# Rounding, routing and turned maxima reordered in a one-core attention and mixture-of-experts kernel

## The chip, the core and the metric

The kernel runs on one core of one Trainium2 chip. A core has five engines that run beside each other, each in the order of its own queue: PE (TensorE, matrix products and transposes), DVE (VectorE), ACT (ScalarE), POOL (GpSimd) and SP (which here only issues transfers). They hand work to each other through semaphores. SBUF is the working memory, PSUM the small memory that PE writes to.

The metric is the device time of one execution in microseconds (us), as the median of several. The profile comes from one execution of its own.

## What is computed

The input is `x`, 16 sequences of 256 tokens with 128 channels, 4096 tokens in all. Cut to what matters:

```python
xn = layernorm(x)                                  # over the 128 channels, eps 1e-5
# attention on xn: 16 heads of 8 channels
Q, K, V = relu(xn @ Wq + bq), relu(xn @ Wk + bk), relu(xn @ Wv + bv)
key_mask = sign(abs(sum(xn, -1)))                  # 0 where the channels sum to exactly 0
scores = einsum(Q, K) / sqrt(8)
scores = where(key_mask == 0, NEG, scores); scores = where(causal, scores, NEG)
a = softmax(scores) * key_mask_of_the_query
o = a @ V + xn
attn = gamma * (o - mean(o)) / sqrt(var(o) + 1e-8) + beta
# experts on xn: 8 experts, 448 hidden channels, the best two per token
h = rms_weight * xn * rsqrt(mean(xn * xn) + 1e-6)
top_w, top_i = top_k(softmax(h @ gate_w.T), 2)     # renormalised over the two
moe = xn + sum over the two of top_w * (silu(h @ w1.T) * (h @ w3.T)) @ w2.T
out = x + attn + moe
```

The mask asks whether a sum of 128 normed values, in the reference's own rounding, is exactly zero. So the kernel must know the normed values bit by bit for it, as an exactly rounded quotient.

## The kernel before, in words

**Tiles and blocks.** 128 tokens are a tile (32 of them, `NT`), four tiles are a block (8 of them, `NB`), which is two sequences. `y` (L103) holds first the input, then the centred input, then the exactly rounded quotient, and at last the attention's output; `xn` (L102) holds the normed values.

**The order of the work.** PE's order is the order of the program, since PE is scheduled by hand (L98). For DVE, ACT and POOL the compiler's scheduler orders the instructions at compile time: an instruction that is ready by its model may be placed ahead of one that stands earlier in the program.

**Norm.** Means are summed in `mean_of` (L306), for the first block on DVE, for the others on POOL. `normed` (L317) works on three chunks of 4, 12 and 16 tiles (L78): it centres on ACT (L325), squares and sums by a scan on DVE (L332, L334), takes a square root by Newton steps (L259), scales on ACT (L361), and refines the root (L365 to L382).

**Exact rounding.** `exact` (L385) makes the rounded quotient of a block from split products: it cuts the value in two halves (L398 on DVE; L401 on `eng`), forms three products by twelve ACT instructions (L407), the residue on DVE (L412), adds the products (L417 on `eng`), and corrects (L421 on DVE). `eng` is DVE for block 0 and POOL for the others. Then it sums the channels of all its blocks in the reference's order (`lane_sum`, L283), and writes the masks `off_all` and `on_all` (L427, L428). It is called for block 0, block 1, and then for pairs of blocks.

**Routing.** `logits` (L548) transposes `xn` and multiplies by the gate. `route` (L432) ranks the experts of each token, finds each token's place in its expert's list, and writes the rows to lists in HBM by indirect DMAs from POOL (L536), 64 in all, in three waves of 16, 8 and 8 tiles (L79). `planned` (L819) computes which expert tile of 256 rows is worked when.

**Attention.** `projected` (L569) makes K, Q and V of a block. The first product into K's PSUM tile is followed by one with `diag` (L579 on ACT, L584 on PE), a diagonal of the mask, so K of a block needs that block's mask. A unit is one block and half its heads, 16 units in all (L619). `scores` (L621) forms the scores in three parts (PE L635, L648), and DVE reduces each to its maxima (L658, L666). `queries` (L680) transposes the maxima and adds them to Q (PE L685, DVE L687, ACT L690, the tile `Qm`). `weights` (L695) forms the scores again, transposed and shifted (PE L710, L723), and ACT takes the exponential (L731). `values` (L734) multiplies by V (PE L743, L754; copied by ACT L764), `finish` (L767) divides and adds (DVE L776 to L810).

**Experts.** `experts` (L900) works 36 tiles in the main part; each fetches 256 rows of a list and its weights through SP (L924 to L934) and takes four steps: two `up` (PE L952, ACT L960, DVE L961 and L963), `down` (PE L969, ACT L977) and `deliver` (PE L983, DVE L985, two indirect DMAs from POOL at L989).

**The main loop** (L1110) traces unit u in an order written out by hand: weights of u, scores of u+1, values and finish of u, and between them six calls of `fill` (L1087). A `fill` advances the generator `prepared` (norm, exact rounding and routing, L1059) by three steps or up to a PAUSE, the projection of the next block by `k_next` steps, the experts by 1.55 steps in the mean (from unit 3 on, L83), and the closing norm (`rest`, L1029) by one. At the end of a unit come `values` of the second sequence, `queries` of the next unit, and `finish`; the next unit's first weights follow directly. After the loop the left experts and the closing norm are worked (L1151 to L1157), and the experts' results are fetched back and added (L1173 to L1185). The pool `psM` (L121) has two PSUM buffers that the projections, logits, transposes, values and expert results share; `psS` (L120) has six for scores, weights and the experts' `up`.

Of the kernel before, what the change touches and what calls it, by code (L numbers as in the profile page):

```python
# [26 lines left out]
def tile_attention_plus_moe(  # L27
# [55 lines left out]
    EARLY_STEPS, EXPERT_STEPS, EXPERTS_FROM = 3, 1.55, 3  # L83
# [233 lines left out]
    def normed(t0, t1):  # L317
# [60 lines left out]
        ninv = small.tile([P, nt], F32, tag="ninv", name=f"ninv_{n}")  # L378
        V.reciprocal(ninv, root)
        V.tensor_scalar(ninv, ninv, -1.0, None, ALU.mult)  # L380
        rhi, rlo = high_low(root[:], nt, "quot")
        roots[t0] = rhi, rlo, ninv  # L382
        yield

    def exact(c0, t0, t1, eng):  # L385

        rhi, rlo, ninv = roots[c0]
        n = f"x{t0}"  # L390
        for b in range(t0, t1, BT):
            bs = slice(b, b + BT)
            q, d = xn[:, bs, :], y[:, bs, :]
            i0 = b - c0
            qh = norm.tile([P, BT, C], F32, tag="qh", name=f"qh_{b}")
            ql = norm.tile([P, BT, C], F32, tag="ql", name=f"ql_{b}")
            r = norm.tile([P, BT, C], F32, tag="r", bufs=2, name=f"r_{b}")
            V.tensor_scalar(  # L398
                qh.bitcast(U32), q.bitcast(U32), HI_BITS, None, ALU.bitwise_and
            )  # L400
            eng.tensor_tensor(ql, q, qh, ALU.subtract)  # L401
            ps = []
            for k, (half, by) in enumerate(((qh, rlo), (ql, rhi), (ql, rlo))):
                p = norm.tile([P, BT, C], F32, tag=f"p{k}", name=f"p{k}_{b}")
                for t in range(BT):
                    i = i0 + t
                    S.activation(p[:, t, :], half[:, t, :], AF.Copy, scale=by[:, i : i + 1])  # L407
                ps.append(p)
            yield
            for t in range(BT):  # L410
                i = i0 + t
                V.scalar_tensor_tensor(  # L412
                    r[:, t, :], qh[:, t, :], rhi[:, i : i + 1], d[:, t, :], ALU.mult, ALU.subtract
                )
            yield
            for p in ps:
                eng.tensor_tensor(r, r, p, ALU.add)  # L417

            for t in range(BT):
                i = i0 + t  # L420
                V.scalar_tensor_tensor(  # L421
                    d[:, t, :], r[:, t, :], ninv[:, i : i + 1], q[:, t, :], ALU.mult, ALU.add
                )
            yield
        tot = small.tile([P, t1 - t0], F32, tag="tot", name=f"tot_{n}")
        yield from lane_sum(tot, y[:, t0:t1, :], t1 - t0, f"s{n}", V)
        V.tensor_scalar(off_all[:, t0:t1], tot, 0.0, None, ALU.is_equal)  # L427
        V.tensor_scalar(on_all[:, t0:t1], off_all[:, t0:t1], -1.0, 1.0, ALU.mult, ALU.add)  # L428
        exact_upto[0] = t1 // BT
        yield  # L430
# [138 lines left out]
    def projected(n):  # L569
# [6 lines left out]
        diag = qkv.tile([P, BT, P], BF16, tag="diag", name=f"diag_{n}")  # L576
# [4 lines left out]
        for r in range(NR):  # L581
# [15 lines left out]
            yield  # L597
            qp = misc(f"q_ps_{n}_{r}")
            T.matmul(qp, lhsT=wq_sb[:, r, :], rhs=xnT, start=True, stop=True)
            QT = qkv.tile([P, BW], F32, tag="QT", bufs=2, name=f"QT_{n}_{r}")  # L600
            S.activation(QT, qp, AF.Relu, bias=qb_sb[:, r : r + 1], scale=QSCALE)
            state[n, r] = (QT, KT, KTm)
            yield
        for b in range(2):
# [16 lines left out]
    def scores(u, part):  # L621
# [21 lines left out]
        for g in range(NG):  # L643
# [13 lines left out]
            if part == 2:  # L657
                V.tensor_reduce(  # L658
# [5 lines left out]
                )  # L664
            else:
                V.tensor_reduce(  # L666
# [5 lines left out]
                )  # L672
# [22 lines left out]
    def weights(u, part):  # L695
# [22 lines left out]
        for g in range(NG):  # L718
# [12 lines left out]
            S.activation(e[:, g, :], sp[g], AF.Exp)  # L731
# [327 lines left out]
    def prepared():  # L1059

        routed = 0
        for a, z in CHUNKS:
            eng = V if a == 0 else G
            yield from normed(a, z)

            first = min(a + BT, z) if a < 2 * BT else a
            if first > a:
                yield from exact(a, a, first, eng)
# [10 lines left out]
            for b in range(first, z, 2 * BT):  # L1079
                yield from exact(a, b, min(b + 2 * BT, z), eng)  # L1080

    exact_upto = [0]
    early_work = prepared()
    side = {"experts": iter(()), "rest": iter(()), "next": iter(())}
    due = [0.0]

    def fill(k_next=1):  # L1087

        for _ in range(EARLY_STEPS):
            if next(early_work, None) is PAUSE:  # L1090
                break
        for _ in range(k_next):
            next(side["next"], None)
        due[0] += EXPERT_STEPS
        while due[0] >= 1:
            next(side["experts"], None)
            due[0] -= 1
        next(side["rest"], None)
# [6 lines left out]
    for _ in projected(0):  # L1105
        pass
# [3 lines left out]
    for u in range(len(units)):  # L1110
        n, r = units[u]
        more = u + 1 < len(units)
        if r == 0 and n + 1 < NB:
            while exact_upto[0] < n + 2:
                next(early_work)
            side["next"] = projected(n + 1)
# [3 lines left out]
        fill()  # L1120
        if more:
            if r == 1:
                while (units[u + 1]) not in state:
                    next(side["next"])
            scores(u + 1, 0)
        fill()
        weights(u, 1)
        fill()
        if more:
            scores(u + 1, 1)  # L1130
        fill(r)
# [3 lines left out]
        fill(r)  # L1135
        weights(u, 2)
        finish(u, 0, o0)
        fill(r)
        if r == 1:
            for _ in side["next"]:  # L1140
                pass
        o1 = values(u, 1)
        if more:
            queries(u + 1)
# [93 lines left out]
```

## Time and profile before

| what | before |
|---|---|
| time, median of 3 runs | 728.03 us (725.95 to 730.34) |
| time of the profiled execution | 728.52 us |
| its span | 726.7 us |
| mean granted PE clock | 0.916 |
| busy: PE, PE weight loads | 566.6 us (78%), 339.6 us (47%) |
| busy: DVE, ACT, POOL | 459.8 (63%), 324.2 (45%), 251.3 us (35%) |
| DMA, mean | 70 GB/s, 50.82 MB |
| share of the chain that ended last: PE, DVE, ACT, POOL | 52%, 20%, 8%, 7% |

The span is the time from the first to the last record of the profiled execution; its own time is measured around it. Busy time is the union of an engine's instructions. The page cuts the span into 40 slices and shows for each the busy tenths of an engine. The clock is the share of full speed that PE was granted. A wait is named by the waiting engine and line and by the line that released it. The chain follows the last instruction back, at each step to what released it.

### The profile page before, as it was taken

The page shows a single profiled execution, that of the slowest core. Times are in us where ns is not written, and L with a number is a line of the kernel's source. Part 1 is how long each engine was busy: PE and PEld are TensorE (multiplying, and loading weights), DVE is VectorE, ACT ScalarE, POOL GpSimd, SP SyncE. Part 2 cuts the span into 40 slices and gives each one's busy share as a digit, 9 for nine tenths or more (in the row PEclk, how much of TensorE's full clock was granted, in tenths as well). Part 3 has the DMA queues.
Part 4 walks back from the last instruction along what each step waited for, and adds up shares of the span by engine and source line. Part 5 has one row for each costly group of instructions (what it writes and reads, how often), then busy time and mean ns, then how long its engine had stood idle before and what let it go on. Part 6 is the DMA issues. An engine that isn't in the chain of part 4 may idle for free.

```text
span 726.7 us, 10435 instructions
## 1 busy us (share of the span) xinstructions
PE 566.6 (78%) x3387; PEld 339.6 (47%) x3401; DVE 459.8 (63%) x1236; ACT 324.2 (45%) x708; POOL 251.3 (35%) x321
## 2 busy tenths in 40 slices
PE   0128778489587898989898989898989899898950
PEld 0013434244354555655455655565555565566740
DVE  5999878976257776655367736564576564637425
ACT  1557755334431634443444553544364444344310
POOL 8404634268814856521121411221142112213630
PEclk9995558889978999999999999999999999999985
DMA  6000000011160225422132211321222122223319
GB/s 160 1 0 0 1 0 1 0 38 38 44 197 27 76 77 147 129 75 67 40 95 64 68 53 54 104 70 45 69 63 83 53 64 75 81 68 91 105 41 329
DMA packets 40761, 50.82 MB, mean 70 GB/s; under 512 B 5925, under 2 KB 33073, under 8 KB 40705
## 3 DMA queue, kind: packets, MB, share of 16 engines
q1 hardware_dynamic: 32128, 38.11, 18.1%
q0 software_dynamic: 4352, 8.47, 3.6%
q10 hardware_dynamic: 4224, 3.55, 1.6%
q8 instruction: 28, 0.46, 0.3%
q14 instruction: 29, 0.23, 0.1%
HBM read 38.35 MB, written 12.27 MB: 70 GB/s over the span
## 4 chain that ended last, share of the span: by engine, by line
PE 52%; DVE 20%; ACT 8%; POOL 7%; issue 6%; DMA 5%; another core or an unknown queue 0%; DVEq 0%; SPq 0%; POOLq 0%; ACTq 0%
PE A L952 7%; PE Y L969 7%; PE G L952 7%; PE S L635 6%; PE W L710 6%; PE O L743 4%; PE W L723 4%; PE S L648 3%; POOL lists L536 3%; ACT e L731 2%; ACT Qm L690 2%; DVE tops L666 2%; DVE y L421 2%; PE O L754 2%; DVE r L412 2%
## 5 line engine op out<-in xcount | busy, mean ns | idle before, releaser
L989 POOL DMA_INDIRECT places<-fres,frows x72 | 70.5, 979 | 272.1 <-DVE fres L985 234.7
L731 ACT ACTIVATE e<-W 128x512 f32<-128x512 f32 x192 | 99.0, 601 | 64.1 <-PE W L723 64.1
L961 DVE SCALAR_TENSOR_TENSOR th<-th,A 112x512 f32<-112x512 f32 x72 | 49.1, 683 | 93.9 <-ACT th L960 93.9
L666 DVE TENSOR_REDUCE tops<-S 128x2 f32<-128x512 f32 x128 | 79.3, 681 | 20.4 <-PE S L648 20.2
L710 PE MATMUL W<-Qm,KT 32*128 32x512 f32 (+1 forms) x512 | 63.0, 569 | 27.8 <-ACT Qm L690 25.2
L952 PE MATMUL A<-hT,w 128*112 128x256 f32 x288 | 78.2, 395 | 7.9 <-ACT hT L943 6.8
L635 PE MATMUL S<-KTm,QT 32*128 32x256 f32 (+1 forms) x512 | 73.3, 560 | 6.0 <-DVE tops L666 4.9
L952 PE MATMUL G<-hT,w 128*112 128x256 f32 x288 | 75.5, 385 | 0.0
L969 PE MATMUL Y<-hid,w 112*128 112x256 f32 x288 | 70.5, 388 | 0.4 <-DVE hid L963 0.4
L536 POOL DMA_INDIRECT lists<-rows_c,ratu_c x64 | 62.4, 975 | 18.5 <-issue 14.4
L960 ACT ACTIVATE th<-A 112x512 f32<-112x512 f32 x72 | 43.4, 602 | 46.6 <-PE A L952 46.6
L952 PEld LDWEIGHTS A<-hT,w 128*112 128x112 f32 x288 | 48.8, 181 | 25.5 <-ACT hT L943 11.0
L969 PEld LDWEIGHTS Y<-hid,w 112*128 112x128 f32 x288 | 54.5, 194 | 11.4 <-issue 1.9
L952 PEld LDWEIGHTS G<-hT,w 128*112 128x112 f32 x288 | 52.0, 181 | 11.8
L764 ACT COPY oT<-O 128x512 f32<-128x512 f32 x32 | 18.8, 586 | 78.1 <-PE O L754 78.1
L963 DVE TENSOR_TENSOR hid<-th,G 112x512 f32<-112x512 f32 x72 | 49.4, 686 | 6.5 <-PE G L952 0.6
L710 PEld LDWEIGHTS W<-Qm,KT 32*128 32x128 f32 x512 | 25.5, 200 | 43.9 <-ACT Qm L690 28.8
L635 PEld LDWEIGHTS S<-KTm,QT 32*128 32x128 f32 x512 | 32.5, 196 | 26.3 <-issue 10.9
L417 POOL TENSOR_TENSOR r<-r,p 128x512 f32<-128x512 f32 x21 | 28.1, 1337 | 43.0 <-DVE r L412 19.5
L658 DVE TENSOR_REDUCE tops<-S 128x4 f32<-128x512 f32 x64 | 39.7, 682 | 3.7 <-PE S L648 3.6
L723 PE MATMUL W<-cmask,ident_bf 128*128 128x256 bf16 (+1 forms) x192 | 41.8, 346 | 0.0
L743 PE MATMUL O<-e,vstat 128*32 128x512 f32 x256 | 38.0, 619 | 2.0 <-ACT hT L943 0.8
(240 smaller groups left out, 880.9 us busy)
## 6 DMA issues: line engine op xcount, KB each, us to landing
w<-in_w1T_dram SPq DMA_DIRECT2D x36, 224.0 KB, 2.6
w<-in_w3T_dram SPq DMA_DIRECT2D x36, 224.0 KB, 3.5
w<-in_w2T_dram SPq DMA_DIRECT2D x36, 224.0 KB, 3.5
frows<-lists SPq DMA_DIRECT2D x36, 130.0 KB, 2.0
x<-in_x_dram SPq DMA_DIRECT2D x8, 256.0 KB, 4.0
z<-places ACTq DMA_DIRECT2D x4, 512.0 KB, 9.4
z<-places SPq DMA_DIRECT2D x4, 512.0 KB, 10.2
lists<-filling SPq DMA_DIRECT2D x9, 130.0 KB, 4.1
```

What stands on the lines that cost most here:

```text
L536: ins = G.indirect_dma_start(out=lists, out_offset=bass.IndirectOffsetOnAxis(ap=at_u[:, r, b + t : b + t + 1], axis=0), in_=rows[:, t, :], ...
L635: T.matmul(out, lhsT=QT[rows, q0 : q0 + P], rhs=KTm[rows, :, b * SEQ : b * SEQ + nk], start=(part < 2 or b == 0), stop=False, skip_group_c ...
L666: V.tensor_reduce(top[:, part, 1, cols], sp[g].rearrange("p (j k) -> p j k", j=HG), AX.X, ALU.max, negate=True,)
L710: T.matmul(out, lhsT=KT[rows, k0 : k0 + P], rhs=Qm[rows, :, k0 : (b + 1) * SEQ], start=(part > 0 or b == 0), stop=False, skip_group_check= ...
L723: T.matmul(out, lhsT=ident_bf, rhs=cmask[:, 1, :].unsqueeze(1).to_broadcast([P, 4 if part == 0 else 2, P]), start=False, stop=True, skip_g ...
L731: S.activation(e[:, g, :], sp[g], AF.Exp)
L743: T.matmul(op[rows, :], lhsT=v[:, 2 * b, r * NG + g, :], rhs=e0[:, g, :], start=True, stop=False, skip_group_check=True, tile_position=(0, ...
L952: T.matmul(to[:, ts(c, SL)], lhsT=wt[:, 0, ts(2 * k + c, CI)], rhs=hT, start=True, stop=True,)
L961: V.scalar_tensor_tensor(th, th, 1.0, ap, ALU.add, ALU.mult)
L963: V.tensor_tensor(h, th, gp, ALU.mult)
L969: T.matmul(yp, lhsT=w2[:, 0, c, :], rhs=hid[c // 2][:, ts(c % 2, SL)], start=(c == 0), stop=(c == NCI - 1),)
L989: ins = G.indirect_dma_start(out=places, out_offset=bass.IndirectOffsetOnAxis(ap=rows[:, a, C : C + 1].bitcast(U32), axis=0), in_=res[:, a ...
```

## The change

It has five parts. (1) `exact` works one block at a time, wholly on DVE and ACT, in eight steps, and forms sum and mask of each block by itself; block 0 still comes first, blocks 1 to 7 are a separate generator `masks`, advanced by two steps a `fill` as soon as their norm is traced, and brought up to block n+1 in unit (n, first half) after the first `values`. The roots that it reads are kept in constants. (2) `beside` traces steps of `prepared` and `masks` inside `tc.issue_after(...)`: each DVE or ACT instruction of such a step is ordered after the last one noted in `behind`, which is the last reduction of `scores` on DVE and the last exponential of `weights` on ACT (at first the last of `exact(0)`). (3) `projected` forms Q ahead of K and of the mask's diagonal; its steps are spread over the two units of a block by the list `due_next`. (4) `queries` of the next unit stands ahead of `values` of the second sequence, with a seventh `fill` after them. (5) The experts take 1.65 steps a `fill`, from unit 4 on.

```diff
-    EARLY_STEPS, EXPERT_STEPS, EXPERTS_FROM = 3, 1.55, 3
+    EARLY_STEPS, EXPERT_STEPS, EXPERTS_FROM = 3, 1.65, 4
...
-    def exact(c0, t0, t1, eng):
...
+    behind = {}
+
+    def exact(n):
+        bs = ts(n, BT)
+        q, d = xn[:, bs, :], y[:, bs, :]
+        by = [roots[n * BT + t] for t in range(BT)]
...
+        V.tensor_scalar(qh.bitcast(U32), q.bitcast(U32), HI_BITS, None, ALU.bitwise_and)
+        V.tensor_tensor(ql, q, qh, ALU.subtract)
+        yield
+        ps = []
+        for k, (half, j) in enumerate(((qh, 1), (ql, 0), (ql, 1))):
+            p = norm.tile([P, BT, C], F32, tag=f"p{k}", name=f"p{k}_{n}")
             for t in range(BT):
+                ins = S.activation(p[:, t, :], half[:, t, :], AF.Copy, scale=by[t][j]).ins
+            ps.append(p)
+        if n == 0:
+            behind["ACT"] = ins
+        yield
+        for t in range(BT):
+            V.scalar_tensor_tensor(
+                r[:, t, :], qh[:, t, :], by[t][0], d[:, t, :], ALU.mult, ALU.subtract
+            )
+        yield
+        for p in ps:
+            V.tensor_tensor(r, r, p, ALU.add)
+        yield
...
+        for k, _ in enumerate(lane_sum(tot, d, BT, f"s{n}", V)):
+            if k % 4 == 3:
+                yield
+        V.tensor_scalar(off_all[:, bs], tot, 0.0, None, ALU.is_equal)
+        ins = V.tensor_scalar(
+            on_all[:, bs], off_all[:, bs], -1.0, 1.0, ALU.mult, ALU.add
+        ).ins
+        if n == 0:
+            behind["DVE"] = ins
+        exact_upto[0] = n + 1
+        yield
...
+        QT = q_of(0)
+        diag = qkv.tile([P, BT, P], BF16, tag="diag", bufs=1, name=f"diag_{n}")
...
+            if r + 1 < NR:
+                QT = q_of(r + 1)
+                yield
...
+        behind["DVE"] = ins
...
+            ins = S.activation(e[:, g, :], sp[g], AF.Exp).ins
+        behind["ACT"] = ins
...
+            normed_upto[0] = z // BT
+            if a == 0:
+                yield from exact(0)
...
+    masks = chain(*(exact(n) for n in range(1, NB)))
...
+    def beside(work):
+        with ExitStack() as order:
+            for ins in behind.values():
+                order.enter_context(tc.issue_after(ins))
+            return next(work, None)
+
+    def fill(k_next=0, k_masks=2):
         for _ in range(EARLY_STEPS):
-            if next(early_work, None) is PAUSE:
+            if beside(early_work) is PAUSE:
                 break
+        for _ in range(k_masks):
+            if exact_upto[0] < normed_upto[0]:
+                beside(masks)
...
-    for _ in projected(0):
-        pass
+    for k, _ in enumerate(projected(0)):
+        if k > 3:
+            beside(early_work)
...
+        due_next = [0, 0, 0, 0, 1, 1, 1] if r == 0 else [1, 1, 1, 1, 0, 0, 0]
...
         o0 = values(u, 0)
-        fill(r)
+        if r == 0 and n + 1 < NB:
+            while exact_upto[0] < n + 2:
+                beside(masks if normed_upto[0] > n + 1 else early_work)
+            side["next"] = projected(n + 1)
+        fill(due_next[4])
         weights(u, 2)
         finish(u, 0, o0)
-        fill(r)
-        if r == 1:
-            for _ in side["next"]:
-                pass
-        o1 = values(u, 1)
         if more:
             queries(u + 1)
+        fill(due_next[5])
+        o1 = values(u, 1)
         exps.pop((u, 0))
+        fill(due_next[6])
         finish(u, 1, o1)
```

## The prediction

> **What bounds the kernel now.** I read the slices of the span first, then the busy time by stage, the waits, the chain that ended last, and single unit ends in the timeline. A unit is one pass over one block and half its heads; sixteen follow each other, and a unit starts when its Qm is written.
>
> The slices (18.2 us each) show three stages. PE is nearly idle for 55 us, then busy at half to 0.9 clock until about 200 us, then busy 8 to 9 tenths at full clock until 700 us, and 26 us of result fetching follow.
>
> ```profile
> PE   0128778489587898989898989898989899898950
> DVE  5999878976257776655367736564576564637425
> PEclk9995558889978999999999999999999999999985
> ```
>
> By stage, with sums of 100, 40 and 349 us (start:end, length, then busy PE, PEld, DVE, ACT, POOL and the clock):
>
> ```profile
> 60.00:160.00 100.00, 74.06 (x337) 37.53 (x341) 85.25 (x240) 54.88 (x153) 43.72 (x38) 0.69 0.02 5
> 160.00:200.00 40.00, 29.59 (x218) 15.31 (x212) 17.64 (x50) 18.98 (x35) 32.73 (x46) 0.97 0.13 42
> 285.00:634.00 349.00, 319.72 (x2060) 192.55 (x2069) 200.80 (x461) 163.41 (x323) 81.02 (x79) 0.98 0.26 75
> ```
>
> From 60 to 160 us DVE is the busy engine (85%); from 285 us PE is (92%). The waits (total, times, longest) name the holes:
>
> ```profile
> PE W L710 <- ACT Qm L690: 25.2, 15, 6.0
> PE k_ps L584 <- ACT diag L579: 18.2, 1, 18.2
> PE hT_ps L941 <- DMA frows<-lists: 7.8, 1, 7.8
> ```
>
> The first comes at every unit's end, 16.4 us in twelve times after 230 us: PE waits 1.4 us for the turned maxima. The second is the start: the first K matmul needs the mask column. The chain says why that is late; between two links of the mask's sum stand squares and scans of later blocks:
>
> ```profile
> 42.35 0.14 DVE lacc_sx L290
> 42.48 0.08 DVE yv_c L349
> 42.56 1.13 DVE xn L334
> 43.69 0.08 DVE lh_sx L294
> 43.77 0.08 DVE yv_c L350
> 43.86 0.59 DVE sq_c L332
> ```
>
> [...] the trace has 677 ns for the adds of L417 on DVE, and 1337 ns on POOL. [...] L421 takes 334 ns at best, 596 ns in the mean and 1417 ns at worst, always beside a POOL add. [...]
>
> **Prices of the stages.** Qm starts at 78.70, 135.30, 165.88, 187.80, 243.10 and 284.84 us (units 0 to 5), and at 633.61 us for unit 15. So units 5 to 14 take (633.61-284.84)/10 = 34.9 us. In the tail an expert tile takes 6.22 us (682.20, 688.42, 694.64 are starts of successive Y). A unit carries 6 fills x 1.55 / 4 = 2.33 tiles = 14.5 us, so attention alone is 20.4 us; unit 2 without experts took 21.9. Check: 243.1 + 12 x 20.4 + 33.7 tiles x 6.22 + 25.5 us from the last yT to the end = 723.0; 3.7 us are left over to the span of 726.7.
>
> **The change, part by part.**
>
> *Mask of block 0 undisturbed.* The sum and mask of L288 to L427 took from 36.03 to 46.68 us. The same sum alone, for the mean, ran from 4.46 to 7.07 us; with one mask operation 2.8 us. Gain 7.9 us, and 1.0 us at L417, whose adds waited behind a scan (31.14 to 32.88): the diagonal starts near 37.8 instead of 46.7 us. From there to the first scores were 10.9 us. Q placed first hides its matmul (-1.5), vb no longer waits 2.2 us in DVE's queue, the logits' transposes and matmuls now stand there (+3): 10.2, hence 48.0 us. From the first scores to Qm were 21.1 us, in which reductions, minima and Qs stood 5.8 us behind norm work: 15.3. Unit 0 starts near **63 us** instead of 78.7.
>
> *What is put off.* The norm of blocks 1 to 7 filled DVE from 30 to 62 us; it now falls into units 0 to 3, at three steps a fill. I count what those units must do on DVE, back to back as the chain shows it, and, as upper end, with the latencies of single instructions. Attention, each unit: 12 reductions x 0.60, rows of finish 1.8, norm sums 1.1, Qs, KTm, vb 1.4: 11.5 to 12.9 us. The norm of blocks 1-3: three squares and scans x 1.74 + some 35 small ones: 11 to 12.8; of blocks 4-7: 13.5 to 15. Exact rounding, a block: 0.34 + 1.05 + 1.05 + sum and mask 2.0 = 4.4, and what comes from POOL, 0.60 + 3 x 0.65 = 2.55: 7.0 to 7.7; at two steps a fill 5.5 blocks are done by unit 4: 38.5 to 42. Routing of 16 tiles 12 to 13.8, of 8 tiles 7 to 8, two plans 7 to 8, logits 0.6. Sum 136 to 152, taken **144 us**. At 0.87 busy (0.85 before, less the holds by POOL) that is 166 us. PE has 4 x 20.4 + 13 for logits = 95 us at full clock; at 0.69 that is 138, so it fits beside. Unit 4 starts at 63 + 166 = **229 us**; before it was 243.1, with 2.3 tiles done.
>
> *POOL to DVE.* POOL loses 28 operations (28.1 + 8.9 us), DVE gains 7 x 2.55 = 17.9 us, counted above. What it saves is DVE time held: L412 and L421 are 12 us over 64 x 0.31, the ranks' L455 to L457 about 3, single small ones some 7. This is why 136 to 152 us are enough for what took longer.
>
> *Routing queued behind.* Every instruction traced beside waits in DVE's or ACT's order for the last reduction or exponential. Behind the waiting ones stand PE's transposes of the next block (in order on PE) and the two shared PSUM buffers, which are freed by lraw (PE stood 3.0 us on it at 105 us). That is in the 0.87. On POOL the 32 list writes with their rows took from 149.97 to 199 us; the weights of the rows are now due in the fourth fill of unit 1, near 130 us, so the lists stand at about 180. SP's first fetch is queued at unit 4, 229 us: the 7.8 us wait goes, and its cover is 50 us. The second and third wave are due in units 3 and 4, the tiles that read them (9 and 17) in units 7 and 9.
>
> *Maxima one group ahead.* A fill and the second values matmuls (3.5 us) now stand between queries and the unit's first weights. The chain from PE to Qm is 2.8 us (319.15 to 321.95), so it is covered; if Qs stood behind a full group of reductions (2.48 us), just so. With oT's wait of 0.4 us, which the last fill covers, a unit loses 1.8 us: **18.6 us**.
>
> *Seven fills of 1.65.* 2.89 tiles a unit; 12 units hold 34.7, so all tiles cost PE 6.22 us as before and only the place moves. The last norm, which lay under 40 us of tiles, lies under 8 us now: bounds 0 and 4 us, taken 0, since the z fetch of 5 us follows. Buffers of one for r and diag, and constants for the roots, cost nothing: their readers are done a unit earlier, else 0.4 us a block.
>
> *Sum.* 229 + 12 x 18.6 + 36 x 6.22 + 25.5 + 3.7 + 7 = 712. The 7 us are unit 4, where DVE has about 44 us (attention 12, tiles 9, 1.5 blocks 11, routing 12) against 36.6 of PE. The profiled run took 728.52 with a span of 726.7, so 1.8 us lie around it: **714 us**; that run is 0.5 us over the median.
>
> **Rivals.**
> 1. The start is given back. With single-instruction latencies (152 us) and 0.85 busy the first units take 179 us, unit 4 starts at 242: 727 us, no change. For it: DVE idles from 37 to 63 us, where it worked before. Against: no holds by POOL.
> 2. Slower. PE stays at half clock while DVE is full, each waiting for the other in order, and experts begin a unit later, so nothing else fills PE. Units of 50 us (unit 0 took 56.6) put unit 4 at 263: 748 us. It decides from 184 us for units 0 to 3 on. Against: most of unit 0's length was norm work of all blocks and POOL holds.
> 3. The order does not do what it says: the compile-time order moves early work or finish before Qs, and the 1.8 us of 12 units stay (+22): 736 us.
>
> **How the numbers follow.** My forecast has 0.58, its own range 695 to 724 (142 to 176 us for units 0 to 3). Rival 1 has 0.17, rival 2 0.18, rival 3 0.07. A measurement tells about 0.5% from no change, 3.6 us. Faster: the forecast and a quarter of rival 1, 0.62; same: the rest of rival 1, 0.13; slower: 0.25. The range, 694 to 740, leaves out most of rival 2 and 0.04 below.
>
> **What would show it.** Right: the first diagonal near 38, Qm of unit 0 near 63 and of unit 4 near 229 us; no wait of W for Qm beyond 5 us in total; DVE over 85% busy from 63 to 200 us; L421 near 340 ns; steady units near 18.6 + 2.89 x 6.22 = 36.6 us. Wrong: unit 4 after 247 us, or PE waits of the same size under another name at a unit's end.

## The result and the profile after

The changed kernel takes **733.79 us** (median of 7 runs) where the kernel before takes 729.70 beside it: a ratio of **1.0058, interval 1.0034 to 1.0083**. It is slower by 0.6%; the forecast was 714 us. Timed twice more beside the kernel before it stood at 1.0084 [1.0059, 1.0109] and 1.0059 [1.0036, 1.0081]. The time lies inside the prediction's whole range of 694 to 740 us, but that range held no change and a loss too, so it says nothing for the mechanism.

The profiled run took 733.07 us, with a span of 731.4 us, 4.7 us over the span before. Its slices (18.3 us each) answer to those shown before.

```profile
PE   0277695773865778999999899999997999998930
DVE  4856879699698793656375745664557546563535
PEclk9998686786897688999999999999999999999975
```

PE starts earlier (0, 2, 7 at the left where 0, 1, 2 stood), and DVE does less in the first slices (4, 8, 5, 6 where 5, 9, 9, 9 stood). But from the fourth slice to the sixteenth, some 290 us, the clock stays between 0.6 and 0.9; before, it was at 0.8 or more from the seventh on but for one slice. The table by stage (start:end, length, then busy PE, PEld, DVE, ACT, POOL and the clock) says it in numbers. First come two stages of the kernel before that were not shown above,

```profile
0.00:60.00 60.00, 11.77 (x34) 4.96 (x34) 49.71 (x185) 26.14 (x76) 25.00 (x84) 0.98 0.20 49
200.00:285.00 85.00, 71.66 (x428) 44.92 (x429) 62.77 (x206) 33.63 (x70) 43.71 (x52) 0.91 0.32 94
```

and then the changed kernel:

```profile
0.00:60.00 60.00, 20.46 (x82) 10.49 (x82) 37.85 (x113) 17.19 (x41) 23.27 (x82) 0.97 0.19 49
60.00:160.00 100.00, 75.09 (x397) 37.92 (x399) 81.80 (x268) 52.03 (x134) 28.29 (x36) 0.76 0.04 14
160.00:200.00 40.00, 26.74 (x141) 13.17 (x140) 33.02 (x98) 22.03 (x56) 20.19 (x24) 0.71 0.08 27
200.00:285.00 85.00, 59.80 (x332) 34.45 (x334) 69.12 (x256) 37.67 (x91) 48.96 (x58) 0.80 0.31 93
285.00:634.00 349.00, 326.57 (x2064) 205.08 (x2072) 203.47 (x462) 164.19 (x329) 75.76 (x72) 1.00 0.27 77
```

In the first 60 us DVE works 37.85 us, where it worked 49.71 before. From 160 to 200 us it works 33.02 instead of 17.64, and the clock is 0.71 instead of 0.97. The work put off has arrived there.

Among the waits (total, times, longest) the two that the change aimed at have shrunk: 2.1 us for Qm (25.2 before) and 7.4 us for the diagonal (18.2 before). Others have come or grown (A waited 6.8 us for hT before).

```profile
PE A L970 <- ACT hT L961: 14.2, 12, 2.5
...
PE lT_ps L571 <- DVE Qs L704: 7.6, 1, 7.6
...
PE S L651 <- DVE tops L682: 7.5, 2, 4.0
PE k_ps L602 <- ACT diag L597: 7.4, 1, 7.4
...
PE pos_ps_c L494 <- DVE rmine_c L480: 6.5, 2, 3.4
```

The starts of the units say where the time went. Qm of unit 0 starts at 58.7 us (63 forecast) and that of unit 4 at 221.0 (229). But from unit 1 on the change itself moves Qm: it is written within the unit before, and the unit's first weights start 5 to 11 us after it, where they started 1.4 us after it before. So the table goes by the first weights (PE W) of each unit; the forecast's Qm is taken 1.4 us later, and its end is what its sum of 712 us leaves.

| from, to | before, us | after, us | forecast, us |
|---|---|---|---|
| start to first weights of unit 0 | 80.7 | 60.1 | 64.4 |
| units 0 to 3 | 163.8 | 165.8 | 166 |
| unit 4 | 41.8 | 60.3 | 43.6 |
| unit 5 | 35.7 | 39.2 | 36.6 |
| units 6 to 14, each | 34.8 | 37.4 | 36.6 |
| first weights of unit 15 to the end | 91.8 | 69.5 | 72.0 |

The first weights of unit 5 start at 286.1 us in the changed kernel and at 286.2 before: the start's 20 us are gone. And the changed kernel has done one unit's share of tiles, 2.89, where the kernel before has done two of 2.33: 1.76 tiles fewer, which at 6.22 us are 11.0 us of PE. So **by unit 5 the start has been given back, and 11 us more**. Units 5 to 14 win some 8 us of that back (27.0 us more for 5.6 more tiles, or 35 us), and the end loses some 2.

Unit 4 is the first with tiles. In the kernel before that was unit 3, and it took 55.3 us there, so part of the length has only moved. The two, the kernel before first:

```profile
189.18:244.48 55.30, 39.92 (x231) 24.79 (x232) 29.71 (x100) 18.15 (x37) 26.99 (x37) 0.85 0.29 87
225.82:286.07 60.25, 42.67 (x224) 25.26 (x224) 45.91 (x157) 23.91 (x53) 33.01 (x38) 0.77 0.40 118
```

Of the 60.3 us PE is busy 42.7, at a clock of 0.77, and waits 17.6, most of it here:

```profile
PE hT_ps L959 <- DMA frows<-lists: 5.0, 1, 5.0
PE top_ps L702 <- DVE fres L1003: 4.3, 1, 4.3
PE pos_ps_c L494 <- DVE rmine_c L480: 3.4, 1, 3.4
PE A L970 <- ACT hT L961: 3.1, 2, 2.5
```

At the end the closing norm lies open. In the trace from 700 us on, the norm's last step on DVE (L1061) comes 1 us before the last yT, that on ACT (L1067) ends 2.7 us after it starts; POOL's four passes take turns with the places of the last tile, and the fetch of the results (L1202) is issued 0.6 us after the last of these passes ends and 3.2 us after the last places (1.3 us in the kernel before, where no pass follows them).

```profile
700.72 0.17 DVE L1061 SCALAR_TENSOR_TENSOR nm<-mv,l_r 128x8 f32<-128x8 f32 x1
...
701.85 0.37 ACT L995 COPY yT<-Y 128x256 f32<-128x256 f32 x1
702.12 2.42 ACT L1067 ACTIVATE y<-y,nm,l_r 128x128 f32<-128x128 f32 x6
...
706.98 0.99 POOL L1007 DMA_INDIRECT places<-fres,frows  x1 [0.17 <-issue]
...
709.35 1.26 POOL L1069 TENSOR_TENSOR y<-y,xn 128x512 f32<-128x512 f32 x1
711.18 2.64 ACTq L1202 DMA_DIRECT2D z<-places  x4
```

From the last yT to the end are 29.5 us; before they were 25.8 (from 700.95 to 726.7).

### The profile page after: what moved, and what is told of

The parts are those of the page before. It is cut to its first block, busy times and chain, and to the rows that moved or that the text cites. A ratio compares the mean times of both kernels' runs of the same rounds, so it can differ in the third digit from the quotient of the medians.

```text
span 731.4 us, 10468 instructions
## 1 busy us (share of the span) xinstructions
PE 570.6 (78%) x3389; PEld 342.1 (47%) x3401; DVE 471.7 (64%) x1303; ACT 323.0 (44%) x708; POOL 219.8 (30%) x293
## 4 chain that ended last, share of the span: by engine, by line
PE 56%; DVE 27%; ACT 9%; DMA 4%; issue 3%; POOL 0%; DVEq 0%; ACTq 0%; POOLq 0%; SPq 0%
PE A L970 8%; PE Y L987 8%; PE G L970 7%; PE S L651 6%; PE W L727 6%; PE O L761 4%; DVE tops L682 4%; ACT e L748 3%; PE S L664 3%; PE W L740 3%; PE O L772 2%; DVE tops L674 2%; PE q_ps L588 2%; PE k_ps L601 1%; DMA y<-in_x_dram 1%
## 5 line engine op out<-in xcount | busy, mean ns | idle before, releaser
L970 PE MATMUL A<-hT,w 128*112 128x256 f32 x288 | 79.1, 398 | 16.3 <-ACT hT L961 14.2
L544 POOL DMA_INDIRECT lists<-rows_c,ratu_c x64 | 66.8, 1044 | 18.5 <-issue 14.5
L727 PE MATMUL W<-Qm,KT 32*128 32x512 f32 (+1 forms) x512 | 65.6, 542 | 2.1 <-ACT Qm L707 2.1
L651 PEld LDWEIGHTS S<-KTm,QT 32*128 32x128 f32 x512 | 33.2, 200 | 29.7 <-DVE tops L682 9.5
L664 PE MATMUL S<-cmask,ident_bf 128*128 128x256 bf16 (+1 forms) x192 | 38.9, 328 | 0.0
L740 PE MATMUL W<-cmask,ident_bf 128*128 128x256 bf16 (+1 forms) x192 | 37.6, 319 | 0.0
L727 PEld LDWEIGHTS W<-Qm,KT 32*128 32x128 f32 x512 | 27.9, 194 | 19.5 <-issue 10.0
```

Of the source, the lines that this page charges most:

```text
L544: ins = G.indirect_dma_start(out=lists, out_offset=bass.IndirectOffsetOnAxis(ap=at_u[:, r, b + t : b + t + 1], axis=0), in_=rows[:, t, :], ...
L651: T.matmul(out, lhsT=QT[rows, q0 : q0 + P], rhs=KTm[rows, :, b * SEQ : b * SEQ + nk], start=(part < 2 or b == 0), stop=False, skip_group_c ...
L664: T.matmul(out, lhsT=ident_bf, rhs=cmask[:, 0, :].unsqueeze(1).to_broadcast([P, 4 if part == 2 else 2, P]), start=False, stop=True, skip_g ...
L727: T.matmul(out, lhsT=KT[rows, k0 : k0 + P], rhs=Qm[rows, :, k0 : (b + 1) * SEQ], start=(part > 0 or b == 0), stop=False, skip_group_check= ...
L740: T.matmul(out, lhsT=ident_bf, rhs=cmask[:, 1, :].unsqueeze(1).to_broadcast([P, 4 if part == 0 else 2, P]), start=False, stop=True, skip_g ...
L970: T.matmul(to[:, ts(c, SL)], lhsT=wt[:, 0, ts(2 * k + c, CI)], rhs=hT, start=True, stop=True,)
```

## The experiments

The theory: the start's gain is real, but it is bought by putting DVE work off into a stage in which PE and DVE wait for each other; with tiles only from unit 4 and an end without cover, it is given back. The rivals: the additions moved from POOL to DVE eat the gain; the maxima one group ahead bring as many waits as they take; the order behind attention costs by itself. The five groups ran on different chips. The kernel before took 729 to 731 us on two of them and 758 to 765 us on three, so only ratios to the kernel before, and times within one group, are compared. Between the two kinds of chip a ratio can differ too, by 0.6 to 0.9% between the changed kernel (1.0058 to 1.0084 on the faster kind) and its nearest relative on the slower (0.9997, the second run below).

### First group: single parts (kernel before: 764.14 us)

**Tiles from unit 3**, at about as many tiles in the units as in the changed kernel:

```diff
-    EARLY_STEPS, EXPERT_STEPS, EXPERTS_FROM = 3, 1.65, 4
+    EARLY_STEPS, EXPERT_STEPS, EXPERTS_FROM = 3, 1.52, 3
```

> The changed kernel with the expert tiles begun in unit 3 again, at 1.52 steps a fill, so that as many tiles as in the changed kernel are left behind unit 15. Theory: the start's gain is real and is given back because PE has no tile to work on until unit 4; the 2.66 tiles of unit 3 take 16.5 us of PE out of the stage in which PE is full, and cost unit 3 what they cost DVE, 2.66 x 3.1 = 8 us: about 725 us. Rival (the operations moved from POOL to DVE are the cause, DVE is full): unit 3 grows by all that is saved later, 733 to 735 us.

Measured: 762.28 us, 0.9979 [0.9968, 0.9991].

**The first fetch ahead of the second wave:**

```diff
+        if u == 3:
+            tiles = experts(ffn_pool, 0, USUAL)
+            next(tiles)
         if u == EXPERTS_FROM:
-            side["experts"] = experts(ffn_pool, 0, USUAL)
+            side["experts"] = tiles
...
         got = {i: fetch(i) for i in range(i0, min(i0 + 2, i1))}
+        yield
```

> The changed kernel with the fetch of the first two tiles traced at the start of unit 3, ahead of the second wave's list writes; the tiles' own steps still begin in unit 4. Theory: the first fetch waits for writes it does not read; without that PE's 5.0 us wait for the rows and most of the 2.5 us at the first A go: 728 to 730 us. Rival (unit 4 is set by DVE anyway, and the wait is hidden under it): 733 to 734 us, with the same idle time of PE under DVE names.

Measured: 763.56 us, 0.9997 [0.9981, 1.0013]. The fetch is issued at 179 us, and no wait for rows is left. But the next run, which leaves the fetch where it was, has no such wait on this chip either, since unit 4 starts later here (240.7 us). So this run says little; the 5.0 us that PE waits for the first rows in the changed kernel stay unpriced. As the nearest to the changed kernel in this group it serves as its stand-in: tiles from unit 3 gain 1.3 us on it, not 9. With the order in place, early tiles do not help, against the theory.

**Fewer tiles in the units:**

```diff
-    EARLY_STEPS, EXPERT_STEPS, EXPERTS_FROM = 3, 1.65, 4
+    EARLY_STEPS, EXPERT_STEPS, EXPERTS_FROM = 3, 1.45, 4
```

> The changed kernel with 1.45 steps a fill instead of 1.65: 30.5 tiles in the units and 5.5 behind them, as before the change. Theory: the closing norm of the last blocks is covered by tiles again, the fetch of the results is issued within 6 us of the last yT, not 9: about 729 us, the sum of units 4 to 15 and of the last tiles unchanged. Rival (the end is set by something else, such as the transfers themselves): 733 to 735 us.

Measured: 759.70 us, 0.9964 [0.9944, 0.9984], 3.9 us under the stand-in. The trace shows the cover back: no closing norm stands behind the last yT.

```profile
731.10 0.37 ACT L995 COPY yT<-Y 128x256 f32<-128x256 f32 x1 [2.93 <-PE Y L987]
...
733.99 0.98 POOL L1007 DMA_INDIRECT places<-fres,frows  x1 [0.30 <-issue]
736.31 2.80 ACTq L1202 DMA_DIRECT2D z<-places  x4
```

The fetch follows the last yT by 5.2 us, not 9.3, and the end by 25.9 us (29.7 in the stand-in). The closing norm's exposure costs some 4 us.

**The maxima alone**, on the kernel before:

```diff
+        if more:
+            queries(u + 1)
         fill(r)
+        o1 = values(u, 1)
+        exps.pop((u, 0))
+        fill(r)
         if r == 1:
             for _ in side["next"]:
                 pass
-        o1 = values(u, 1)
-        if more:
-            queries(u + 1)
-        exps.pop((u, 0))
         finish(u, 1, o1)
```

with 1.33 steps a fill, so that seven fills carry as many tiles as six did.

> The kernel before with one part alone: the maxima of the next unit turned one group ahead and a seventh fill, at 1.33 steps (9.3 steps a unit, as before). Theory: this part works, the 16 to 25 us of W waiting for Qm go and some 0.6 us a unit come back under other names: 712 to 719 us. Rival (the seventh fill and the earlier maxima bring as many waits at the two shared PSUM buffers): 726 to 731 us, no change.

Measured: 738.21 us, **0.9672 [0.9641, 0.9703]**. The part works, and the rival of equal new waits falls. The gain is larger than expected: 712 to 719 us, worked out for a chip with 729, are 0.977 to 0.986.

### Second group: parts taken away (kernel before: 729.08 us)

> The changed kernel itself, timed beside the others of this group, since the chip of the first group took 764 us for the kernel before, 36 us more than the chip of the result. If the chips only scale, 1.006 of the kernel before; if the slower chip lengthens the stage before unit 5 more in one kernel than in the other, 0.995 to 1.000, as the nearest variants had there.

Measured: the changed kernel, 734.73 us, 1.0084 [1.0059, 1.0109].

**The additions back on POOL:**

```diff
-        V.tensor_tensor(ql, q, qh, ALU.subtract)
+        eng = V if n == 0 else G
+        eng.tensor_tensor(ql, q, qh, ALU.subtract)
...
-            V.tensor_tensor(r, r, p, ALU.add)
+            eng.tensor_tensor(r, r, p, ALU.add)
```

> The changed kernel with ql and the three adds of blocks 1 to 7 put back on POOL, the rest as it is: 7 x 2.6 = 18 us less on DVE, 7 x 5.3 = 37 us more on POOL, and POOL's holds of DVE back. Rival (this move off POOL is what eats the gain): 10 us or more faster than the changed kernel. Theory (DVE is full but so are the waits around it, and the holds return): within 4 us of the changed kernel.

Measured: 768.93 us, **1.0557 [1.0531, 1.0584]**, 34 us slower than the changed kernel. Neither side had expected a loss. One line of DVE's groups from 60 to 310 us shows why (busy us and mean ns, then the idle time ahead of it):

```profile
L424 DVE SCALAR_TENSOR_TENSOR y<-r,ninv_c,xn 128x128 f32<-128x128 f32 x28 | 9.5, 380 | 46.9 <-POOL r L420 46.9
```

DVE stands idle for 46.9 us ahead of these corrections, in five waits for POOL's additions, and runs no reduction of attention in that time. But the additions themselves are not what is long. Three of the five waits make up 41.8 us, and in them POOL works on the rows and list writes of the routing that stand ahead of the additions in its own queue. The longest is 16.0 us; POOL's three additions (L420) are its last 4:

```profile
290.97 1.04 POOL L538 TENSOR_TENSOR rows_c<-xn,rstd 128x512 f32<-128x512 f32 x1
...
296.15 0.96 POOL L545 DMA_INDIRECT lists<-rows_c,ratu_c  x1 [0.30 <-issue]
297.13 3.96 POOL L420 TENSOR_TENSOR r<-r,p 128x512 f32<-128x512 f32 x3
```

With the rounding spread into the stage of the list writes, the move to DVE saves 34 us; the rival falls.

**Without the order behind attention:**

```diff
-        with ExitStack() as order:
-            for ins in behind.values():
-                order.enter_context(tc.issue_after(ins))
-            return next(work, None)
+        return next(work, None)
```

> The changed kernel without the order that queues early work behind the last reduction and exponential. Theory (the work itself is what fills the stage, not its order): within 5 us of the changed kernel, either way. Rival (PE stands because transposes and logits wait for queued DVE work in order): 8 us or more faster, the waits of the logits' and lT's PSUM buffers for Qs (12.9 us) gone.

Measured: 717.94 us, **0.9865 [0.9831, 0.9899]**, 16.8 us faster than the changed kernel and faster than the kernel before. The rival won. By first weights unit 4 starts 9.0 us earlier than in the changed kernel of this group and takes 54.5 us instead of 60.3. Qm of unit 0 comes at 73.42 us, 15.2 later than with the order (58.25), but that of unit 4 at 211.81, 8.6 earlier, and of unit 6 at 300.59, 14.8 earlier. DVE works 49.56 us in the first 60, as before the change. The waits named in the expectation shrink to 3.5 us: 1.9 for the logits and 1.6 for lT.

**Without the rounding of blocks 1 to 7:**

```diff
-        V.tensor_scalar(qh.bitcast(U32), q.bitcast(U32), HI_BITS, None, ALU.bitwise_and)
-        V.tensor_tensor(ql, q, qh, ALU.subtract)
+        if n == 0:
+            V.tensor_scalar(qh.bitcast(U32), q.bitcast(U32), HI_BITS, None, ALU.bitwise_and)
+            V.tensor_tensor(ql, q, qh, ALU.subtract)
```

and so for its products, residues, additions and corrections: the mask of these blocks is then not the exact one.

> The changed kernel without the exact rounding of blocks 1 to 7: their mask is taken from the sum of the unrounded rows, which leaves out some 7 x 5 = 35 us of DVE and 7 x 3 us of ACT in units 0 to 5. Theory (DVE is what these units last): 22 to 30 us faster than the changed kernel. Rival (PE at a low clock and the waits in order set these units): under 12 us faster.

Measured: 710.73 us, 0.9748 [0.9722, 0.9773], 24.0 us faster than the changed kernel, within the theory's 22 to 30. The load does count in these units: DVE is busy 38.3 us less in the whole run (433.6 for 471.9), and 24 of them come back as time. ACT is busy 24.6 us less as well, and the run does not tell the two apart.

### Third group: combinations (kernel before: 757.86 us)

> The kernel before with the maxima one group ahead and a seventh fill alone, again, beside the others of this group. On the first chip it took 0.967 of the kernel before; if this holds on a faster chip, 705 us; if part of it was that chip's longer stage before unit 5, 710 to 715 us.

Measured: the maxima alone again, 736.11 us, 0.9705 [0.9673, 0.9738]. In PE's waits from 280 to 640 us none for Qm ahead of W is left; what came in its place at Qs and Qm is small:

```profile
PE hT_ps L941 <- DVE Qs L687: 2.3, 3, 0.8
...
PE O L743 <- ACT Qm L690: 1.8, 3, 0.6
```

**No order, tiles from unit 3 at 1.33 steps:** the edit of the run without the order, and the tiles' start of the very first run, at a lower rate.

> The changed kernel without the order behind attention, and with tiles from unit 3 at 1.33 steps a fill, so that 5.7 tiles cover the closing norm and the first fetch is traced ahead of the second wave. Theory: without the order 718 us; the end gives 4 us, the first fetch up to 6, the early tiles some more: 705 to 711 us. Rival (these waits hide each other): 715 to 718 us.

Measured: 733.53 us, 0.9681 [0.9648, 0.9715]. The ratio is 1.8% under that of the kernel without order, which ran on a faster chip (0.9865). Of that, 0.6 to 0.9% can be the chip; what is left, about 1%, speaks for the theory that these waits add, and does not show it.

**Maxima ahead, and the additions on DVE**, on the kernel before, beside the edit of the maxima alone:

```diff
-            eng = V if a == 0 else G
+            eng = V
```

> The kernel before with the maxima one group ahead, and the additions of the exact rounding (ql and the three adds) on DVE instead of POOL, nothing put off and nothing ordered. Theory (the move to DVE is a gain also where nothing is queued, POOL's holds of DVE and its slow adds in the chain go): 4 to 12 us less than the maxima alone. Rival (it pays only in the changed kernel's order, 18 us more on a full DVE here): 5 to 15 us more.

Measured: 716.20 us, **0.9435 [0.94, 0.9471]**, 20 us under the maxima alone, more than the theory's 4 to 12. Nothing is put off and nothing ordered here, and the move to DVE is a gain by itself. This kernel beats both.

**The order behind unit 0 only:** the reductions update `behind` in unit 0's scores alone, the exponentials never.

> The changed kernel with early work queued only behind unit 0's scores (and block 0's rounding), no longer behind the newest reduction and exponential of later units. If the start's gain is real and only the later order eats it, unit 0 stays at 58 us and units 0 to 3 take 138 us as without the order: unit 4 at 196, about 703 us. If the start is zero-sum (11 us of DVE work is only moved out of 37 to 60 us into a stage that DVE fills), unit 4 at 208 to 215 and 714 to 720 us, as without any order.

Measured: 746.57 us, 0.9856 [0.9819, 0.9892]. Unit 0 stays early (59.5 us), and Qm of unit 4 comes at 224.8 us. The times expected were worked out from a faster chip, on which the changed kernel reaches unit 4 20 us earlier than its relative does on a slower one (221.0 against 240.7), so this start decides nothing. The ratio does: the first case's 703 us are 0.964 of the kernel before on that chip, and the measured ratio lies 2% above that, more than the chips make. The first case falls. The ratio of the kernel without any order (0.9865) is met, as the second case has it.

### Fourth group: one part each on top of the best kernel (kernel before: 764.66 us)

> The kernel before with the maxima ahead and the additions on DVE, again, as the base of this group. 0.944 of the kernel before as on the first chip that ran it, within 0.005; 0.95 to 0.965 if part of that gain was that chip's.

Measured: 719.06 us, 0.9401 [0.9359, 0.9443]; the base of this group.

**The projection:** the changed kernel's `projected`, with Q first, and its list `due_next` of steps, put into the base.

> The base of this group with the changed kernel's projection: Q ahead of the mask's diagonal and of K, and its steps spread as the changed kernel has them. If the later steps bring the waits of q_ps for Qs and nothing else, 2 to 5 us more than the base; rival (the start's Q first saves as much), within 2 us.

Measured: 725.36 us, 0.9505 [0.9475, 0.9536], 6.3 us more than the base. Units 5 to 14 are 0.7 us longer each from Qm to Qm (339.6 us against 332.4), 0.4 us by first weights, and a wait that the base has nowhere stands among PE's from 285 to 660 us:

```profile
PE q_ps L580 <- DVE Qs L695: 4.1, 5, 1.0
```

**The order alone:**

```diff
-            if next(early_work, None) is PAUSE:
+            if beside(early_work) is PAUSE:
```

with `behind` set in `scores` and `weights` as the changed kernel does, and `beside` at the place too that brings the masks up to the next block.

> The base of this group with early work queued behind the newest reduction and exponential, the order alone. Theory (the order costs what e6 gave back, by DVE standing where the compile-time schedule would have placed work, and PE behind it): 12 to 20 us more than the base, unit 0 as early as in the base or earlier. Rival (the order costs only where the rounding is also put off): within 5 us.

Measured: 736.84 us, 0.9654 [0.9619, 0.9689], 17.8 us more than the base. The stages of the base (start:end, length, busy PE, PEld, DVE, ACT, POOL, clock),

```profile
0.00:60.00 60.00, 13.62 (x36) 5.58 (x36) 49.46 (x188) 27.09 (x79) 23.79 (x83) 0.97 0.19 49
60.00:140.00 80.00, 67.47 (x324) 33.98 (x329) 73.08 (x241) 53.02 (x146) 14.49 (x18) 0.73 0.03 11
...
290.00:345.00 55.00, 51.88 (x338) 31.60 (x339) 30.50 (x70) 28.09 (x57) 9.78 (x10) 1.00 0.26 74
```

and of the base with the order:

```profile
0.00:60.00 60.00, 20.85 (x86) 11.59 (x90) 39.99 (x116) 19.57 (x49) 22.69 (x82) 0.96 0.20 49
60.00:140.00 80.00, 51.92 (x314) 25.69 (x319) 58.87 (x199) 39.12 (x96) 25.33 (x33) 0.76 0.06 17
...
290.00:345.00 55.00, 47.35 (x248) 28.40 (x248) 43.26 (x131) 32.88 (x83) 3.93 (x4) 0.81 0.26 76
```

This is the core of the case. With the order DVE works 98.9 us of the first 140, without it 122.5. From 34 to 140 us it stands ahead of instructions of attention, the projection and the logits, where the base has norm work to do (the same waits there are 0.2 us at KTm, 1.9 at lraw and 0.5 at tops):

```profile
DVE KTm L596 <- ACT KT L593: 7.9, 4, 2.7
DVE tops L659 <- remote: 7.5, 1, 7.5
DVE lraw L557 <- PE logit_ps L556: 4.7, 3, 2.8
DVE tops L667 <- PE S L649: 3.6, 3, 2.5
```

The second of these can't be put down to the order: "remote" means that the trace has no instruction that released it, and from 60 to 345 us such waits of DVE add up to 18.8 us here and to 19.4 in the base. The other three add up to 16.2 us. The work comes back later: from 290 to 345 us DVE has 12.8 us more to do, and there the base has its clock at 1.00 and the ordered kernel at 0.81. Qm of unit 0 is 16.6 us earlier (57.76 against 74.32), of unit 5 1.9 us later, of unit 6 17.5 us later, and so it stays.

**The rate and the start of the tiles:** 1.65 steps from unit 4.

> The base of this group with tiles from unit 4 at 1.65 steps a fill instead of from unit 3 at 1.33. Theory (end uncovered 4 us, A waiting for hT, nothing for PE in unit 3): 8 to 14 us more than the base. Rival (only the place of the tiles moves): within 3 us, as the prediction had it.

Measured: 730.84 us, 0.9579 [0.9538, 0.962], 11.8 us more than the base. By the traces the two are even at unit 5 (10.5 us early, 1.77 tiles or 11.0 us of PE behind), so the late start of the tiles costs nothing. From there on 8.5 us are lost. From Qm to Qm the ten units from 5 to 14 take 38.6 us more, of which 5.6 more tiles are 34.8, and the time from unit 15 to the end is 19.0 us less for 3.8 tiles fewer, or 23.8 us: 3.7 and 4.8 us. By first weights it is 6.1 and 2.4. Behind the last yT 3.0 us are lost (29.5 against 26.5 us).

### Fifth group: the rest (kernel before: 730.61 us)

**The rounding spread block by block**, without order, on the maxima ahead and the additions on DVE: the changed kernel's `exact(n)` and `masks`, two steps a fill.

> The kernel with maxima ahead and additions on DVE, and on top of it alone the rounding spread block by block next to its use, two steps a fill, without order, with the old projection, rate and start of tiles. From the kernel with everything but the order (0.968 at the same rate) less the projection (1.1 per cent): 0.955 to 0.962 of the kernel before, 1.5 to 2.3 per cent more than without it (0.940 to 0.944). Rival (nothing: the projection and its interaction are all of it): 0.940 to 0.948.

Measured: 707.22 us, 0.9693 [0.9671, 0.9715], outside both. Its base ran only on chips of the slower kind, so its ratio can't be set beside this one closely. What its trace has and the base's has not is a wait for the first tiles' rows,

```profile
PE hT_ps L951 <- DMA frows<-lists: 21.2, 2, 20.4
```

20.4 us long, in unit 3, which takes 61.5 us by first weights. What it would be worth to be rid of it was not run.

> The changed kernel. If the parts add up, 0.940 x 1.011 x 1.027 x 1.019 = 0.995 without the rounding's spread and 1.00 to 1.02 with it. On a chip on which the kernel before takes 729 us it took 1.006 and 1.008; nearest to it on a slower chip was 0.9997.

Measured: 734.17 us, 1.0059 [1.0036, 1.0081], 27 us more than the run before it. On this kind of chip the order (16.8 us by the second group) and projection and rate together (by difference 10 us) make that up.

## Why the prediction was wrong

**Mask undisturbed: right.** The diagonal starts at 37.77 us (37.8 forecast), the first scores at 46.6 (48.0), and Qm of unit 0 at 58.7 (63). What the forecast did not see is what it costs. From the mask's last operation (37.9 us) to the first reduction (48.0) DVE is idle 8 of 10 us; the base of the fourth group, with its norm unhindered, has 49.46 us of DVE work in the first 60 where the changed kernel has 37.85.

**Work put off, units 0 to 3: right as a sum.** They took 165.8 us for 166, at a DVE load of 81.80 us in the 100 from 60 to 160. Rival 1, "the start is given back", expected this to fail already here; the loss came in unit 4. That the sum came out is in part luck: it counted the order as no more than the 0.87, and without the order these units take 141.4 us.

**Routing queued behind, and the 7 us of unit 4: the step that failed.** The forecast put the order's whole price "in the 0.87" of DVE's busy share and took its end for unit 4; for what was left of the early work there it added 7 us to the 36.6 of a steady unit. Measured, unit 4 took 60.3 us, 23.7 over 36.6. The order holds DVE's work back behind reductions that wait for PE (7.9 us in three waits from 34 to 140 us, where the kernel before has none), and so the work is not done by unit 4: from 200 to 285 us DVE is busy 69.12 us, where 62.77 were busy before. Removing the order gave 16.8 us back, 9.0 of them net ahead of unit 4 and 5.8 in it; adding it alone to another kernel cost 17.8. That is the greater part of the 19.4 us between the forecast's span and the measured one, and it is shown in both directions. The rest of unit 4 is not the order's: without it the unit still takes 54.5 us. As the first unit with tiles it meets what unit 3 met before, 55.3 us there by first weights, and the prediction's own starts of Qm (187.80 and 243.10 us) have that length. It took its measure from units 5 to 14 instead. Which of its waits could be had back stays open. The lists stood at 180 us, as forecast. But "its cover is 50 us" was wrong: the first fetch is traced behind the second wave's writes too, POOL's last of them was issued at 229.2, the fetch at 231.5, and PE waited 5.0 us.

**POOL to DVE: right in direction, far too small.** Counted as 17.9 us added against some 22 of holds saved. The holds are read from the trace of the kernel before: eight of L421's 32 took 1335 to 1417 ns and four of L412's 32 took 1239 to 1414 ns, each of the twelve with a POOL tensor_tensor (L401 or L417) running beside it for 1.09 us or more; the other 52 took 334 to 353 ns. Why they are longer there was not shown. As a count of DVE's work that was right: on the kernel with the maxima ahead and nothing put off DVE's busy time went from 461.1 to 455.9 us. But the time gained was 20 us there and 34 us in the changed kernel. The term left out is DVE's own wait at POOL's additions, with all that stands behind it: 7.3 us in the kernel before and in the maxima alone, none after the move, and 46.9 us where the additions stand behind list writes. What makes up the rest of the 20 us was not traced. The corrections after the additions take 348 ns in the median and 421 in the mean, because of two of 32 (2002 ns beside POOL's L1055 and 1123 ns beside its L537); L421 had a median of 344 before (336 at best, not 334) and its mean of 596 from the eight long ones, five of them beside an addition (L417) and three beside the subtraction (L401). The "340" came true but for the two.

```profile
L423 DVE SCALAR_TENSOR_TENSOR y<-r,ninv_c,xn x32: 264/348/2002, 33.7 to 267.6; 128x128 f32<-128x128 f32 x32
L421 DVE SCALAR_TENSOR_TENSOR y<-r,ninv_c,xn x32: 336/344/1417, 34.4 to 140.5; 128x128 f32<-128x128 f32 x32
```

**Maxima ahead: right alone, lost in company.** Forecast 21.6 us (12 x 1.8); alone, 22 and 26 us. In the changed kernel a steady unit is 37.4 us, not 36.6. Two parts cost as much by themselves on the base of the fourth group: the projection, with its new wait for the shared PSUM buffer that Qs frees (0.4 to 0.7 us a unit, by first weights or by Qm), and the rate (0.6 to 0.4).

**"All tiles cost PE 6.22 us as before and only the place moves": wrong.** At 1.65 steps a fill PE waits for hT more often: 14.2 us in the whole run, 6.8 before; on the base of the fourth group 9.2 against 5.7. The closing norm "taken 0" was near its upper bound of 4: 3.7 us of the 29.5 behind the last yT.

**The sum.** By first weights the start was 4.3 us better than forecast and units 0 to 3 0.2; units 4 and 5 cost 19.2 more and units 6 to 14 7.2; the end was 2.5 better: 712 + 19.4 = 731.4, the span measured. The profile did show much of what rival 2 said, PE at a low clock and each waiting for the other (in unit 4 a clock of 0.77, with DVE busy 76%). It came later and at a smaller price than its 748 us. The test of rival 2 in units 0 to 3 was set too early: work that is only put off is paid where it ends, not where it starts.

**What stays open.** The price of the rounding spread block by block: 0.9681 against 0.9435 x 1.011 leaves up to 1.5% on the slower chips, while the parts 0.940 x 1.011 x 1.027 x 1.019 = 0.995 without it nearly reach the stand-in's 0.9997; the parts do not simply multiply. The base was not run on the faster kind of chip, so whether it beats 707 us there is unknown. The wait of the first fetch was not priced, neither the 5.0 us in the changed kernel nor the 20.4 in the one with 707 us. Why the first unit with tiles is so long (55.3 us before, 60.3 in the changed kernel, 54.5 without the order) was not taken apart.

## What to carry to other kernels

An order that queues side work behind the critical work makes the critical work early once and leaves the engine idle wherever the critical instruction waits; before adding it, count the idle time of that engine that the side work fills now, here 24 us in 140. An operation moved to a slower engine (an addition of 128x512 took 1337 ns on POOL and 677 on DVE in the kernel before) is priced by the wait of the engine that needs its result, with what stands ahead of it in the slower engine's queue and what stands behind that wait, not by its busy time: 46.9 us of waiting beside 26.9 us of POOL's busy time in the second group. Part-wise runs on one base show which half of a mixed change to keep: here 6% of gain stood beside 6% of loss. And stages of two kernels are compared by a mark that the change does not move: by Qm the changed kernel looks 9.8 us early at unit 5 (275.04 against 284.84), where by its first weights it was level.

## What was not expected of the hardware

The same program differs by chip more than the whole change does: the kernel before took 729 to 731 us in two groups and 758 to 765 in three. Between the changed kernel and its stand-in of the first group the whole difference lies before unit 5: from Qm of unit 0 to that of unit 5 216.4 us on one chip and 244.4 on the other, and 377.6 and 376.5 us for the ten units after it. In that stage (60 to 345 us) the traces of all runs on the three slower chips have waits for which no releaser is on record, 18 to 38 us of ACT and up to 22 us of DVE, single ones as long as 17.7 us; on the faster chips they are 1.5 us at most. What they are was not found.
